# A two-layer attention kernel: v made with seven block products instead of eight

## The chip, the cores and the metric

The kernel runs on one core of a Trainium2 chip. The metric is the device time of one execution in microseconds, the median of three runs.

## The reference

x has the shape (16, 256, 32, 32) in float32: 16 images, C = 256 channels, N = 32 x 32 = 1024 positions. Two layers follow each other, and each adds to x what an attention over the positions makes of the normalised x:

```
x = x + attention(groupnorm(x), Wq, bq, Wk, bk, Wv, bv, rel_h, rel_w)

q, k, v = W @ xf + b                      # xf: (256, 1024); 4 heads of d = 64
sim  = einsum('bhdi,bhdj->bhij', q, k)
qpos = einsum('hdi,bhdj->bhij', rel_h + rel_w, q)
out  = einsum('bhdn,bhmn->bhdm', v, softmax(sim + qpos))
```

The normalisation takes 16 groups along the last axis, over channels and width. Everything is computed in float32.

## The kernel before, in words

A *unit* is one image in one layer; there are 32, in an order that interleaves the two layers. A unit has two pairs of heads (`pr`), and a pair has two halves of 512 queries, so a unit has four *blocks*, called b = 0 to 3 here. `block(n)` (L803) issues the instructions of one block on all engines, in an order written out by hand; each engine runs its own instructions in that order. Blocks with even b also make the projections that come next: b = 0 makes q, k and the second half of v for the unit's own second pair of heads (`w` is the same unit), b = 2 makes q, k and the first half of v for the next unit. A block does this:

- Eight groups of *scores* j = 0 to 7 (`scores`, L549): a tile of 128 keys by 2 heads by 512 queries, four matmuls of 64 rows by 64 columns that use the four quarters of TensorE together. Ahead of each, VectorE writes the *seed* (`seed`, L513), the positional term, into the two PSUM banks that the scores add to. Behind it, ScalarE takes the exponential out of the banks into p (`scores`, L560 and L562).
- The product of p with v (`attend`, L602) in two stretches, one from the lower and one from the upper rows. Its groups j = 0 to 3 read `vts[u, 0]`, j = 4 to 7 read `vts[u, 1]`. `take_out` (L663) copies the result out of PSUM.
- The sums of p over the keys: VectorE adds p tiles into `first` and `acc` (`add_up`, L567, L582), and DMAs that accumulate, issued on GpSimd's queue, add and fold those (`add_first` L619, `fold` L624, `fold_again` L643, `fold_stack` L648, first<-p L578).
- `finish` (L720, L727) normalises an older pair's output and adds it to x.

The PSUM has eight banks, used as four pairs "a" to "d"; `ring` names them `ta, tb, tx, tz` in each block. In an even block `tz` holds q and k, `tx` holds v until it is copied, and the seeds go round over the pairs.

q and k are made together with seven block products instead of eight (`first_product` L360, `two_products` L409) after Winograd's form of Strassen's scheme: the weights' sums are built once (`forms`), the sums of the normalised input x_n once a unit (`input_sums`, L344 to L351). v is made in the plain way: `values` (L445), 64 products of 64 rows by 256 columns a unit, in two stretches of each even block; ScalarE copies them out (L470). A second stretch waits for the end of the first one on TensorE itself (`stretches`). `norms` issues ScalarE's share of the next units' normalisation after tables (`APPLY`, `SQUARES`, `SUMS`), in pieces between the exponentials.

## Time and profile before

| What | Value |
|---|---|
| Median of 3 runs | 2478.74 us (2478.73 to 2479.44) |
| The profiled execution | 2479.26 us, span 2477.5 us |
| TensorE busy | 2467.9 us (100%) |
| VectorE busy | 2350.6 us (95%) |
| ScalarE busy | 2076.5 us (84%) |
| GpSimd busy | 795.7 us (32%) |
| Granted TensorE clock | 0.999 |

A busy time counts the stretches in which at least one instruction of the engine ran; matmuls are pipelined, so the distance from one group's start to the next one's says more than the length of a record. A float32 matmul leaves two records. Weight loads (PEld) run beside matmuls. A record's start on VectorE can lie up to 0.1 us ahead of the end of the one before it. In a row of a timeline stand the start, the length, the engine, the line, the operation, what it writes and reads, and how many instructions were merged; in brackets the idle time ahead of it and what ended it.

### The profile page before, as it was taken

The numbers are of one execution on the slowest core, as the hardware profiler recorded it, in microseconds if no ns is written. First come the engines' busy times: TensorE is split into PE (matmuls) and PEld (weight loads), VectorE is DVE, ScalarE is ACT, GpSimd is POOL, SyncE is SP. The second block draws the span as 40 slices with busy tenths as digits, with TensorE's granted clock in tenths as the row PEclk, the third lists the DMA queues.
The fourth block names the chain that finished last, engine by engine and source line by source line (L and its number), as shares of the span: only waits on it lengthen the run. The fifth ranks groups of instructions, "written<-read, shape, count | busy, mean of one in ns | idle before, by whom it ended". The sixth has DMA issues, their size and how long they took to land.

```text
span 2477.5 us, 86516 instructions
## 1 busy us (share of the span) xinstructions
PE 2467.9 (100%) x37030; PEld 1825.8 (74%) x37030; DVE 2350.6 (95%) x2815; ACT 2076.5 (84%) x4341; POOL 795.7 (32%) x942
## 2 busy tenths in 40 slices
PE   9999999999999999999999999999999999999998
PEld 5777777777777777777777777777777777777785
DVE  8899999999999999999999999999999999999998
ACT  8888888898888888888888889888888888888764
POOL 0233333333333333333333333333333333333231
PEclk9999999999999999999999999999999999999999
DMA  3655655657557566565575665665656656556564
GB/s 95 115 104 98 129 96 114 119 118 144 112 115 144 105 116 118 108 137 112 113 133 108 125 119 99 130 134 109 129 118 135 116 93 131 112 96 121 106 129 116
DMA packets 138551, 289.25 MB, mean 117 GB/s; under 512 B 55848, under 2 KB 57384, under 8 KB 138160
## 3 DMA queue, kind: packets, MB, share of 16 engines
q0 software_dynamic: 72288, 197.74, 47.3%
q1 hardware_dynamic: 65584, 85.38, 11.6%
q8 instruction: 293, 4.80, 0.8%
q14 instruction: 98, 0.80, 0.1%
q10 hardware_dynamic: 288, 0.52, 0.1%
HBM read 51.78 MB, written 17.30 MB: 28 GB/s over the span
## 4 chain that ended last, share of the span: by engine, by line
PE 98%; DVE 1%; ACT 1%; DMA 0%; issue 0%; SPq 0%; PEldq 0%; ACTq 0%
PE banks L549 36%; PE banks L602 35%; PE banks L409 13%; PE banks L445 9%; PE banks L486 2%; PE banks L360 2%; PE banks L317 0%; PE banks L240 0%; DVE banks L513 0%; DMA x<-in_x_dram 0%; ACT p L562 0%; PE banks L675 0%; ACT xn L296 0%; ACT junk L221 0%; DVE r L1121 0%
## 5 line engine op out<-in xcount | busy, mean ns | idle before, releaser
L513 DVE TENSOR_TENSOR banks<-abt 128x1024 f32<-128x1024 f32 x1207 | 1241.2, 1061 | 93.3 <-ACT p L562 49.2
L562 ACT ACTIVATE p<-banks,shift 128x1024 f32<-128x1024 f32 x898 | 981.4, 1116 | 202.5 <-PE banks L549 104.6
L549 PE MATMUL banks<-q,k 64*64 64x512 f32 x8192 | 1068.9, 590 | 0.5 <-DVE banks L513 0.4
L602 PE MATMUL banks<-p,v 64*64 64x256 f32 x16384 | 951.6, 376 | 0.0
L602 PEld LDWEIGHTS banks<-p,v 64*64 64x64 f32 x16384 | 838.5, 133 | 120.4 <-issue 39.1
L549 PEld LDWEIGHTS banks<-q,k 64*64 64x64 f32 x8192 | 466.2, 133 | 281.8 <-issue 153.7
L582 DVE TENSOR_TENSOR acc<-acc,p 128x1024 f32<-128x1024 f32 x381 | 465.2, 1221 | 4.3
L648 POOL DMA_DIRECT2D stack<-stack x310 | 308.2, 994 | 316.8 <-DMA stack<-stack 148.7
L409 PE MATMUL banks<-t,form 64*64 64x512 f32 x1984 | 399.7, 589 | 0.0
L643 POOL DMA_DIRECT2D stack<-acc x248 | 241.6, 1186 | 471.2 <-DMA stack<-acc 458.0
L445 PE MATMUL banks<-Wv,xn 64*64 64x256 f32 x3968 | 293.5, 378 | 0.0
L409 PE MATMUL banks<-xn,form 64*64 64x512 f32 x992 | 258.8, 589 | 0.0
L445 PEld LDWEIGHTS banks<-Wv,xn 64*64 64x64 f32 x3968 | 228.9, 133 | 40.2 <-PEq L199 16.8
L619 POOL DMA_DIRECT2D acc<-first x126 | 115.1, 914 | 423.1 <-DVE acc L582 224.3
L296 ACT ACTIVATE xn<-x,nshift,rstd 128x128 f32<-128x128 f32 x496 | 209.3, 500 | 30.1 <-DVE nshift L289 30.1
L221 ACT ACTIVATE junk<-x,neg 128x128 f32<-128x128 f32 x501 | 199.7, 407 | 0.0
L560 ACT ACTIVATE p<-banks,shift 128x512 f32<-128x512 f32 x252 | 159.8, 685 | 35.3 <-PE banks L549 32.3
L409 PEld LDWEIGHTS banks<-t,form 64*64 64x64 f32 x1984 | 137.8, 133 | 67.8 <-issue 41.8
L624 POOL DMA_DIRECT2D acc<-acc x124 | 103.3, 833 | 254.5 <-DMA acc<-first 251.4
L578 POOL DMA_DIRECT2D first<-p x127 | 114.1, 899 | 179.2 <-ACT abt L499 66.8
L567 DVE TENSOR_TENSOR acc<-p,p 128x1024 f32<-128x1024 f32 x128 | 156.2, 1220 | 0.4 <-DMA acc<-first 0.4
L567 DVE TENSOR_TENSOR first<-p,p 128x1024 f32<-128x1024 f32 x127 | 154.7, 1218 | 0.0
(120 smaller groups left out, 1776.6 us busy)
## 6 DMA issues: line engine op xcount, KB each, us to landing
first<-p POOLq DMA_DIRECT2D x127, 512.0 KB, 6.8
acc<-first POOLq DMA_DIRECT2D x126, 512.0 KB, 5.5
rden<-rd SPq DMA_DIRECT2D x126, 256.0 KB, 6.7
acc<-acc POOLq DMA_DIRECT2D x124, 256.0 KB, 5.9
stack<-acc SPq DMA_DIRECT2D x248, 64.0 KB, 2.9
stack<-acc POOLq DMA_DIRECT2D x248, 64.0 KB, 3.4
out_dram<-x SPq DMA_DIRECT2D x31, 512.0 KB, 2.9
x<-in_x_dram SPq DMA_DIRECT2D x30, 512.0 KB, 9.5
```

Of the source, the lines that this page charges most:

```text
L221: nc.scalar.activation(junk, grouped(xt[units[u][0]], g), func, accum_out=into[:, g : g + 1], **bias)
L296: nc.scalar.activation(grouped(xns[u], g), grouped(xt[units[u][0]], g), AF.Identity, bias=shift[:, g : g + 1], scale=rstd[:, g : g + 1],)
L409: yield nc.tensor.matmul(ps[c, a, :], f[rs, left[a], c0 : c0 + D], right[a][rs, :], start=(t == 0 and step == 1 and a == 1), stop=(t == 1) ...
L445: yield nc.tensor.matmul(pv[c, a, i, :], xns[u][rs, cc, j0 : j0 + D], W.wv[l][rs, cc, :], start=(t == 0 and cc == 0 and i == 0), stop=(t = ...
L513: nc.vector.tensor_tensor(ps[:, h].rearrange("p h (w y) -> p h w y", y=H), ab[:, h, :H].unsqueeze(2).to_broadcast(shape), ab[:, h, H + hal ...
L549: nc.tensor.matmul(ps[c, h, :], a[hs, j0 : j0 + D], b[hs, columns], start=bool(tag) and i == 0, stop=i == len(terms) - 1, skip_group_check ...
L562: nc.scalar.activation(p, ps, AF.Exp, bias=W.shift)
L567: nc.vector.tensor_tensor(t, probs[blk, a], probs[blk, b], ALU.add)
L582: nc.vector.tensor_tensor(accs[blk], accs[blk], probs[blk, j], ALU.add)
L602: yield nc.tensor.matmul(po[c, a, :QUART], vts[u, j // 4][rs, j % 4, c0 : c0 + D], p[rs, h, a * QUART : (a + 1) * QUART], start=(fresh and ...
L643: nc.gpsimd.dma_start(at, acc[R:D, h, :], accum_op=ALU.add)
L648: nc.gpsimd.dma_start(stack[:rows_], stack[rows_ : 2 * rows_], accum_op=ALU.add)
```

## The change

v, too, is made with seven products of blocks of 128 rows. The sums of the weights stand in `vform`, built once a layer by `value_forms`; the sums of the input are those that q and k have already. The products are made in pairs, `value_pair`, and the first one, `odd_products`, together with q's and k's first product. A matmul of v now has 128 columns instead of 256, and there are 112 a unit instead of 64. b = 2 makes the first product and a pair (48 matmuls), b = 0 two pairs (64).

The results need five additions a unit. Two, which read PSUM, are VectorE's: into c22 in b = 0 and into c11 in b = 2. Three are GpSimd's `tensor_tensor`, SBUF only, all in b = 0: into c22, into c12 and into u2; for the last one ScalarE copies a bank into a part of x_n that is no longer read. c12 is read by the product with p of the same block, groups j = 4 to 7; c22 and u2 belong to the second pair of heads and are read two blocks later.

The order in `block` changes around these. The second pair's stretches stand between scores 3, 4 and 5. `tx` holds v longer, so seeds 3 to 6 take turns in `ta` and `tb`, seed 7 goes to `tx`, and p's product with v to `ta`. The exponential of scores 4 is one instruction instead of two halves. The first sum of p (`add_up(blk, 1)`) comes behind v's addition and seed 4. The first sum of the input in b = 2 goes to the head of the block, and the tables `APPLY` and `SQUARES` move pieces of normalisation to later places. The spread reciprocals have one buffer instead of two, to make room.

The core of the diff:

```diff
-            first = None if plain else first_product(w, pr, qk)
-            v, v_out = values(w, 1 - b // 2, psum2(tx, f"pv_{w}_{b}"), first)
+            pv = psum2(tx, f"pv_{w}_{b}")
+            if plain:
+                v, v_out = values(w, 1, pv)
+            elif b == 0:
+                new_values(w, 1)
+                v = value_pair(w, 1, pv, first_product(w, pr, qk))
+            else:
+                v = odd_products(w, pr, qk, pv)
...
-            add_up(blk, 1)
             v(1)
+            if b == 2:
+                new_values(w, 0)
+                nc.scalar.copy(value_block(w, 0, 0), bank_of(pv, 0))
+                after_first(w, pr, qk)
+            elif plain:
+                v_out()
+            else:
+                c22, u2 = value_block(w, 1, 1), value_block(w, 0, 1)
+                nc.scalar.copy(c22, bank_of(pv, 0))
...
-            v_out()
+            seed(blk, 4, tb)
+            if b == 0 and not plain:
+                nc.vector.tensor_tensor(c22, c22, bank_of(pv, 1), ALU.add)
+                nc.gpsimd.tensor_tensor(c22, c22, u2, ALU.add)
+            add_up(blk, 1)
             if n > 0:
                 scores(blk, 3)
-            seed(blk, 4, tb)
...
+                v = value_pair(w, 2 - b, pv)
+            if b == 0:
+                products(0)
+            if not plain:
+                v(0)
+            seed(blk, 5, ta, halves=True)
+            scores(blk, 4)
+            if not plain:
+                v(1)
+            if b == 2:
+                c11 = value_block(w, 0, 0)
+                nc.vector.tensor_tensor(c11, c11, bank_of(pv, 1), ALU.add)
+                nc.scalar.copy(value_block(w, 0, 1), bank_of(pv, 0))
+                products(0)
+            elif not plain:
+                c12 = value_block(w, 1, 0)
+                part = bank_of(xns[w][:, :, :HALF], 0)
+                nc.scalar.copy(c12, bank_of(pv, 0))
+                nc.gpsimd.tensor_tensor(c12, c12, u2, ALU.add)
+                nc.scalar.copy(part, bank_of(pv, 1))
+                nc.gpsimd.tensor_tensor(u2, u2, part, ALU.add)
             norms(u, b, 1)
-            seed(blk, 5, tx, halves=True)
-            scores(blk, 4, halves=True)
-            seed(blk, 6, ta)
+            scores(blk, 5)
+            seed(blk, 6, tb)
+            products(1)
             if folded:
                 stack_up(previous)
-            scores(blk, 5)
-            products(1)
-            po = psum2(tx, f"po_{n}")
+            po = psum2(ta, f"po_{n}")
             zeroed(po)
-            seed(blk, 7, tb, halves=True)
+            seed(blk, 7, tx, halves=True)
...
-    APPLY = {0: (3, 7, 7, 7, 7, 7), 1: (7, 7, 7, 11, G, G)}
+    APPLY = {0: (3, 3, 3, 7, 7, 7), 1: (7, 7, 7, 11, G, G)}
```

Three places show the new order. TensorE at the head of a block b = 0 before, from the first product (L360) on; `Wv` rows are v, `q,k` rows are scores 2, 3 and then 4 and 5, `form` rows are q and k:

```order
L360 MATMUL banks<-xn_16334,form_76 64x512 x2
L445 MATMUL banks<-Wv_78,xn_16334 64x256 x12
L360 MATMUL banks<-xn_16334,form_76 64x512 x2
L445 MATMUL banks<-Wv_78,xn_16334 64x256 x4
L549 MATMUL banks<-q_0_16928,k_0_16929 64x512 x4
L445 MATMUL banks<-Wv_78,xn_16334 64x256 x16
L549 MATMUL banks<-q_0_16928,k_0_16929 64x512 x4
L409 MATMUL banks<-t_16851,form_76 64x512 x2
L409 MATMUL banks<-xn_16334,form_76 64x512 x2
L549 MATMUL banks<-q_0_16928,k_0_16929 64x512 x8
```

The same place in the changed kernel, where `vform` rows are v:

```order
L377 MATMUL banks<-xn_15228,form_76 64x512 x2
L457 MATMUL banks<-vform_78,t_15772 64x128 x12
L377 MATMUL banks<-xn_15228,form_76 64x512 x2
L457 MATMUL banks<-vform_78,t_15772 64x128 x4
L631 MATMUL banks<-q_0_15833,k_0_15834 64x512 x4
L457 MATMUL banks<-vform_78,t_15772 64x128 x16
L631 MATMUL banks<-q_0_15833,k_0_15834 64x512 x4
L426 MATMUL banks<-t_15772,form_76 64x512 x2
L426 MATMUL banks<-xn_15228,form_76 64x512 x2
L457 MATMUL banks<-vform_78,xn_15228 64x128 x2
L457 MATMUL banks<-vform_78,t_15772 64x128 x2
```

Ahead of scores 2 and 3 stand the same numbers of v's matmuls with half the columns; the other pair now follows ahead of scores 4 and 5, which used to come together.

VectorE at that place before, from the last addition of the older block on; `abt` rows are seeds 3, 4, 5 (halves), 6, 7 (halves):

```order
L582 TENSOR_TENSOR acc_1_1_9703<-acc_1_1_9703,p_1_1_7_9667 128x1024
L513 TENSOR_TENSOR banks<-abt_0_9701 128x1024
L567 TENSOR_TENSOR first_0_0_9858<-p_0_0_0_9747,p_0_0_1_9823 128x1024
L513 TENSOR_TENSOR banks<-abt_0_9701 128x1024
L513 TENSOR_TENSOR banks<-abt_0_9701 128x512 x2
L513 TENSOR_TENSOR banks<-abt_0_9701 128x1024
L513 TENSOR_TENSOR banks<-abt_0_9701 128x512 x2
L720 TENSOR_TENSOR od_1_8654<-od_1_8654,rden_1_9650 128x1024
```

And in the changed kernel:

```order
L664 TENSOR_TENSOR acc_1_1_10207<-acc_1_1_10207,p_1_1_7_10171 128x1024
L595 TENSOR_TENSOR banks<-abt_0_10205 128x1024 x2
L962 TENSOR_TENSOR v_1_10322<-v_1_10322,banks 128x4x128
L649 TENSOR_TENSOR first_0_0_10387<-p_0_0_0_10251,p_0_0_1_10327 128x1024
L595 TENSOR_TENSOR banks<-abt_0_10205 128x512 x2
L595 TENSOR_TENSOR banks<-abt_0_10205 128x1024
L595 TENSOR_TENSOR banks<-abt_0_10205 128x512 x2
L807 TENSOR_TENSOR od_1_9105<-od_1_9105,rden_1_10154 128x1024
```

Seed 3 keeps its place; seed 4 moves ahead of the first sum, and v's addition (L962) stands between them.

GpSimd's queue in a block b = 0 before, from `add_first` (L619) to `fold_again` (L643):

```order
L619 DMA acc_1_1_11577<-first_1_1_11534 128x1024
L648 DMA stack_0_11168<-stack_0_11168 8x512
L578 DMA first_0_0_11732<-p_0_0_2_11730 128x1024
L624 DMA acc_1_1_11577<-acc_1_1_11577 64x1024
L648 DMA stack_0_11168<-stack_0_11168 4x512
L643 DMA stack_1_11627<-acc_1_0_11414 32x512 x2
L643 DMA stack_1_11627<-acc_1_1_11577 32x512 x2
```

And in the changed kernel:

```order
L701 DMA acc_1_1_11197<-first_1_1_11154 128x1024
L730 DMA stack_0_10772<-stack_0_10772 8x512
L706 DMA acc_1_1_11197<-acc_1_1_11197 64x1024
L730 DMA stack_0_10772<-stack_0_10772 4x512
L725 DMA stack_1_11246<-acc_1_0_11034 32x512 x2
L963 TENSOR_TENSOR v_1_11311<-v_1_11311,v_0_10860 128x4x128
L660 DMA first_0_0_11376<-p_0_0_2_11345 128x1024
L994 TENSOR_TENSOR v_1_11311<-v_1_11311,v_0_10860 128x4x128
L996 TENSOR_TENSOR v_0_10860<-v_0_10860,xn_10278 128x4x128
L725 DMA stack_1_11246<-acc_1_1_11197 32x512 x2
```

The three additions (into c22, c12 and u2) stand behind the folds of the older block, and the first sum's DMA has moved from ahead of the fold to between the additions.

More of the change, by code (lines that the diff above doesn't have):

```diff
@@ L435, in k_half, with value_part, odd_products, products @@
         )
+    def value_part(u, ps, rs, a, form, right, i, start=False, stop=False):
+        for x, c in enumerate(QUARTERS):
+            p0 = i * P + x * D
+            yield nc.tensor.matmul(
+                ps[c, a, i * P : (i + 1) * P], right[rs, p0 : p0 + D],
+                W.vform[units[u][1]][rs, form, :],
+                start=start and i == 0, stop=stop, skip_group_check=True,
+            )
+    def odd_products(u, pr, qk, pv):
+        f = W.form[units[u][1]]
+        def products(t):
+            mine, other = ((LO, HI), (HI, LO))[t]
+            for i in range(NT // 2):
+                yield from value_part(u, pv, mine, 0, A11, xb(u, 0, 0), i, t == 0, t == 1)
+                if i == 0:
+                    for h, c in enumerate(QUARTERS):
+                        c0 = pr * P + h * D
+                        yield nc.tensor.matmul(
+                            qk[c, 0, :], f[other, A11, c0 : c0 + D], xb(u, 0, 0)[other, :],
+                            start=t == 0, stop=t == 1, skip_group_check=True,
+                        )
+        return stretches(products)
+    def value_pair(u, step, pv, first=None):
+        left, right = (
+            ((S2, A12), (ts[u][:, T2], xb(u, 1, 0))),
+            ((S1, S3), (ts[u][:, T1], ts[u][:, T3])),
+            ((S4, NA22), (xb(u, 1, 1), ts[u][:, T4])),
+        )[step]
+        fresh = (1, 0, 2)[step]
+        def products(t):
+            rounds = [
+                [
+                    value_part(
+                        u, pv, rs, a, left[a], right[a], i, t == 0 and a >= fresh, t == 1
+                    )
+                    for rs, a in BANKS[t]
+                ]
+                for i in range(NT // 2)
+            ]
+            if t == 0 and first is not None:
+                yield from woven(rounds, first)
+            else:
+                for r in rounds:
+                    for p in r:
+                        yield from p
+        return stretches(products)
+    def value_block(u, nh, ch):
+        return vts[u, nh][:, :, ch * P : (ch + 1) * P]
+    def bank_of(ps, a):
+        return ps[:, a, :].rearrange("p (b c) -> p b c", c=P)
+    def new_values(u, g):
+        vts[u, g] = vpool.tile([P, NT // 2, C], F32, tag="v", name=f"v_{u}_{g}")
     def values(u, g, pv, first=None):
@@ L820, in block @@
         ta, tb, tx, tz = ring
+        if even and b == 2:
+            input_sums(w, 0)
         if previous and even:
```

65 lines of the change are left out of this document (44 added, 21 removed).

## The prediction

> **What bounds the kernel now.** I read the page first, then busy time by windows, then the timelines of TensorE (PE), VectorE (DVE), ScalarE (ACT) and GpSimd (POOL) over one steady unit. Busy times, then shares of the chain that ended last:
>
> ```profile
> PE 2467.9 (100%) x37030; PEld 1825.8 (74%) x37030; DVE 2350.6 (95%) x2815; ACT 2076.5 (84%) x4341; POOL 795.7 (32%) x942
> PE 98%; DVE 1%; ACT 1%; DMA 0%; issue 0%; SPq 0%; PEldq 0%; ACTq 0%
> ```
>
> TensorE is the path, and VectorE is right behind it. In a steady window (columns: length, then busy us of PE, PEld, DVE, ACT, POOL):
>
> ```profile
> 1100.00:1400.00 300.00, 300.00 (x4532) 223.28 (x4528) 287.05 (x338) 257.30 (x547) 101.18 (x119) 1.00 0.61 117
> ```
>
> DVE is idle 12.95 us in 300, and the granted clock is 1.00. Now TensorE at the start of a block b=0 (first L360 at 1022.09), then of the b=2 block after it (1060.23); L549 are scores, L445 v, L602 the product with p:
>
> ```profile
> 1021.23 1.07 PE L549 MATMUL banks<-q,k 64*64 64x512 f32 x8
> 1022.09 0.63 PE L360 MATMUL banks<-xn,form 64*64 64x512 f32 x2
> ...
> 1024.67 1.13 PE L549 MATMUL banks<-q,k 64*64 64x512 f32 x8
> 1025.53 2.00 PE L445 MATMUL banks<-Wv,xn 64*64 64x256 f32 x32
> 1027.26 1.13 PE L549 MATMUL banks<-q,k 64*64 64x512 f32 x8
> ...
> 1028.97 1.99 PE L549 MATMUL banks<-q,k 64*64 64x512 f32 x16
> ...
> 1033.27 1.07 PE L602 MATMUL banks<-p,v 64*64 64x256 f32 x14
> ```
>
> ```profile
> 1060.23 0.63 PE L360 MATMUL banks<-xn,form 64*64 64x512 f32 x2
> ...
> 1062.81 1.13 PE L549 MATMUL banks<-q,k 64*64 64x512 f32 x8
> ...
> 1065.40 1.13 PE L549 MATMUL banks<-q,k 64*64 64x512 f32 x8
> ...
> 1071.40 1.46 PE L602 MATMUL banks<-p,v 64*64 64x256 f32 x21
> ```
>
> From start to start, a group of scores takes 0.86 (1024.67 to 1025.53), 32 v records take 1.73 (to 1027.26), and the woven stretch with the first product takes 2.58 (1022.09 to 1024.67). Two blocks are 38.14, so a unit is 76.28, and of that DVE idles 3.3 (76.28 x 12.95/300).
>
> **The change, term by term.** *TensorE.* v has 112 products of 128 columns in a unit for 64 of 256: 7/8 of the columns. In b=0 it stays at two pairs, in two places instead of one; in b=2 it falls by a quarter of the former v, one slot of 0.86. Do 128-column products run at the column rate? The nearest row is shorter still:
>
> ```profile
> 1012.55 0.93 PE banks L486 x61
> ```
>
> A stretch of 64 records of 64 columns takes 0.93, 14.5 ns each; 32 of 128 columns need 0.86, 27 ns each, so issue doesn't limit them. Removed: 0.86 a unit, in 31 units 26.7 us, if nothing else gets late.
>
> *The VectorE total.* Rows by form:
>
> ```profile
> L513 DVE TENSOR_TENSOR banks<-abt 128x1024 f32<-128x1024 f32 x829 | 1002.5, 1227 | 91.9 <-ACT p L562 49.2 <-ACT od L663 41.0 <-ACT abt L499 1.0
> L513 DVE TENSOR_TENSOR banks<-abt 128x512 f32<-128x512 f32 x378 | 246.1, 697 | 1.4 <-ACT v L470 0.9 <-ACT p L560 0.5
> L433 DVE SCALAR_TENSOR_TENSOR k<-banks,bk,k 128x512 f32<-128x512 f32 x124 | 87.2, 703 | 0.0
> L470 ACT COPY v<-banks 128x512 f32<-128x512 f32 x128 | 68.8, 590 | 37.0 <-PE banks L445 37.0
> L562 ACT ACTIVATE p<-banks,shift 128x1024 f32<-128x1024 f32 x898 | 981.4, 1116 | 202.5 <-PE banks L549 104.6 <-DVE rstd L276 83.4 <-PE banks L602 3.3
> ```
>
> The two additions read PSUM and SBUF as L433 does: 2 x 0.70 = 1.4. Of 3.3 idle 1.9 is left, less the 0.86 that the unit would shrink by: 1.0. In total VectorE still fits; what decides is where its work is due.
>
> *Seeds, b=0.* Every group of scores needs a seed that VectorE wrote into its banks. VectorE there:
>
> ```profile
> 1024.85 1.23 DVE L513 TENSOR_TENSOR banks<-abt 128x1024 f32<-128x1024 f32 x1
> 1025.99 1.22 DVE L567 TENSOR_TENSOR first<-p,p 128x1024 f32<-128x1024 f32 x1
> 1027.12 2.43 DVE L513 TENSOR_TENSOR banks<-abt 128x1024 f32<-128x1024 f32 x3
> 1029.70 2.47 DVE L513 TENSOR_TENSOR banks<-abt 128x1024 f32<-128x1024 f32 x3
> 1032.08 1.22 DVE L720 TENSOR_TENSOR od<-od,rden 128x1024 f32<-128x1024 f32 x1
> ```
>
> Seed 3 ends at 1024.85 + 1.23 = 1026.08, and nothing ahead of it on VectorE changes. Scores 3 were due at 1027.26. Both v stretches ahead of them now lose 0.86, so they are due at 1025.53. With about 0.1 for the handover they start at 1026.2: 0.7 late. The products of the second pair now lie behind them, so scores 4 start three slots later, at 1028.8. The second pair of v also keeps the third pair of banks until it is copied, so seeds 3 to 6 alternate over two pairs, and seed 6 must wait for the exponential of scores 4. That wait shows in ACT's idle time:
>
> ```profile
> 1022.36 1.12 ACT L562 ACTIVATE p<-banks,shift 128x1024 f32<-128x1024 f32 x1 [0.27 <-PE banks L549]
> ...
> 1025.87 1.12 ACT L562 ACTIVATE p<-banks,shift 128x1024 f32<-128x1024 f32 x1 [0.25 <-PE banks L549]
> ```
>
> The exponential starts 1.13 to 1.20 after its scores (1021.23, 1024.67). VectorE meanwhile: seed 4 to 1027.4, v's addition (0.7), the first sum (1.22) and seed 5 to 1030.3, with the overlaps of 0.1 between records; scores 5 are due at 1030.5, so those just fit, and VectorE then idles 0.8. On the path instead: scores 4 at 1028.8, exponential 1029.97 to 1031.09, seed 6 to 1032.35. Scores 6, four slots of 0.86 behind scores 4, are due at 1032.2 and start at 1032.45. Seed 7 in halves (0.70 each, overlapping by 0.1) ends at 1033.55; scores 7 were due at 1033.3 and start at 1033.65. The product with p starts at 1034.5 instead of 1033.27: **+1.2 us** (bounds 0.7, the first wait alone, and 1.6, if v's addition, which now waits for a copy on ScalarE with the first sum and seed 5 queued behind it, also makes scores 5 late).
>
> *Seeds, b=2.* VectorE there:
>
> ```profile
> 1062.01 1.22 DVE L513 TENSOR_TENSOR banks<-abt 128x1024 f32<-128x1024 f32 x1
> 1063.14 0.68 DVE L349 TENSOR_TENSOR t<-t,xn 128x512 f32<-128x512 f32 x1
> 1063.74 1.22 DVE L567 TENSOR_TENSOR first<-p,p 128x1024 f32<-128x1024 f32 x1
> ...
> 1067.84 2.48 DVE L513 TENSOR_TENSOR banks<-abt 128x1024 f32<-128x1024 f32 x3 [0.20 <-ACT p L562]
> ```
>
> Seed 3 ends at 1063.23. Three slots from 1060.23 put scores 3 at 1062.81 instead of 1065.40; they start at 1063.35, 0.54 late. Seed 4, which moves ahead of the first sum, ends near 1064.97; scores 4 are due at 1065.07. The addition into c11 (0.70) waits for TensorE's second stretch of the pair, with seed 6 queued behind it; it ends at 1067.9 and seed 6 at 1069.05, with scores 6 due at 1069.37. Nine slots from 1063.35 end at 1071.1; with 0.1 at scores 7 the product with p starts at 1071.2 instead of 1071.40: **-0.2 us** of the 0.86 (bounds -0.5 and +0.1).
>
> *What costs nothing.* ScalarE has one more copy (0.59) a unit and two exponentials whole instead of in halves; by the windows' row it idles 42.70 in 300, 10.9 a unit, which covers it. The normalisations that leave the start of b=0 and b=2 only make room ahead of the exponentials; if they landed in front of one instead, each would cost what it delays. The sum of inputs that moves ahead of an addition on VectorE in b=2 leaves seed 3 where it is. The forms of v are some ten small instructions, once: 1 us. Reciprocals' spread with one buffer on SP's queue waits for a multiplication one block earlier, so nothing queues behind it. The sum's DMA on GpSimd, now issued some 5 us later, is next needed a block later.
>
> *GpSimd's additions.* No row shows one. The bounds are 0.69 (VectorE's of that size) and 1.19 (GpSimd's slowest row, below). The one that matters is the addition into c12, which the product with p reads from its fifth group, after 32 records of 256 columns, 1.73 as v's; behind it on TensorE are the next block's first scores. GpSimd's queue at b=0, and the page's row of its fold:
>
> ```profile
> 1031.49 0.82 POOL L624 DMA_DIRECT2D acc<-acc  x1 [2.84 <-DMA acc<-first]
> 1032.02 1.13 POOL L648 DMA_DIRECT2D stack<-stack  x1
> 1032.56 2.34 POOL L643 DMA_DIRECT2D stack<-acc  x2
> ```
>
> ```profile
> L643 POOL DMA_DIRECT2D stack<-acc x248 | 241.6, 1186 | 471.2 <-DMA stack<-acc 458.0 <-issue 13.2
> ```
>
> Both additions of b=0 and the first-sum DMA are now queued behind these. From between 1033.75 (one row's mean behind the start) and 1034.90, with additions of 0.69 to 1.19 and a DMA issue of 0.54 (the pace of these rows) to 0.82, c12 is ready between 1035.7 and 1038.1; it is needed at 1034.5 + 1.73 = 1036.2. I take nothing for it, nearer to the early end: the 2.84 of waiting at L624 is for a transfer that ran beside the first sum's, and that one now goes out behind it. 1.5 stays for the range.
>
> **Sum.** 31 x (1.2 - 0.2) + 1 = +32 on the profiled execution's 2479.26 (span 2477.5 and 1.76 around it; 0.5 above the median 2478.74). On the median: **2510 us**. This case's own range: 31 x 0.2 to 31 x 1.7, 2486 to 2532.
>
> **Rivals.** *VectorE is held while GpSimd adds.* The three additions fall where VectorE runs seed 7, the normalisation and the next seeds, all with two inputs from SBUF. If such instructions can't run beside an addition of GpSimd, VectorE loses 3 x (0.69 to 1.19) = 2.1 to 3.6 a unit, at a place where it is already late; the cushion behind it is its wait for the copy of the output:
>
> ```profile
> DVE banks L513 <- ACT od L663: 41.0, 60, 1.1
> ```
>
> That is 41.0/60 = 0.7 a time, so 1.4 to 2.9 stay on top of the forecast: 2510 + 43 to 2510 + 90, 2553 to 2600, middle 2576. For it: VectorE's rows stand end to end there. Against it: VectorE's sums keep their length beside GpSimd's DMA work, though that isn't an addition (min, median, max ns):
>
> ```profile
> L582 DVE TENSOR_TENSOR acc<-acc,p x381: 1212/1220/1227, 48.9 to 2449.9; 128x1024 f32<-128x1024 f32 x191
> ```
>
> Chance 0.28. The Trainium skill states such a rule (SBUF — State Buffer, § Who interferes with whom): a VectorE instruction with two SBUF inputs and a GpSimd instruction that reads SBUF exclude each other for a whole instruction. By that rule the time is about 2576; the trace of before has no addition on GpSimd and can't show it. The same skill (GPSIMD Engine Reference, § Performance versus the Vector engine) gives 4497 ns for 2048 elements, by which I estimate 1.1 us for 512.
>
> *c12 comes late.* No holding, but the queue above keeps the product with p waiting 0.5 to 1.5 in each b=0: 2525 to 2556. Chance 0.12.
>
> *Faster.* If seed 3 were ready at 1025.5 and 1062.8, TensorE would keep its order without waits and the whole 0.86 stays: 2478.7 - 26.7 + 1 = 2453. This decides from seeds 0.7 and 0.54 earlier than the trace has them; VectorE's 3.3 idle speaks for it, the unchanged order ahead of seed 3 against it. Partial gains reach 2473. Chance 0.19. *A draw:* the waits come to 0.86, half of the 1.2 + 0.66 that I count, and the time to 2474 to 2484; chance 0.10. That the change doesn't do what it says is out: its matmuls are there in the built order.
>
> **Chances and range.** Forecast 0.31, held VectorE 0.28, late c12 0.12, faster 0.19, draw 0.10. A measurement here can tell about 0.2%, 5 us, from no change. Faster 0.19, same 0.10, slower 0.71. The range from 2460 to 2590 leaves out half of the faster case (0.1) and the upper quarter of the held one (0.07).
>
> **What would show it.** Right: TensorE's wait for L595's seeds at scores 3 of both even blocks, 0.7 and 0.5; an idle VectorE of some 0.8 before seed 6 of b=0; a unit of 77.3. Held VectorE: records of seeds or sums of over 1.5 us beside GpSimd's TENSOR_TENSOR. Late c12: TensorE or its weight loads waiting for v's L994. Wrong: a unit of 75.4 and no wait for seeds.

## The result and the profile after

| | Before | After |
|---|---|---|
| Median | 2479.05 us | 2686.39 us |
| Ratio, with its 95% interval | | 1.083 (1.082 to 1.085) |
| TensorE busy | 2467.9 us (100%) | 2573.9 us (96%) |
| VectorE busy | 2350.6 us (95%) | 2534.0 us (94%) |
| GpSimd busy | 795.7 us (32%) | 946.5 us (35%) |

One of the four executions of the changed kernel took 2926.2 us at a granted clock of 0.873 and is left out of the ratio, though not of the median; the other three took 2685.3 to 2687.5.

The kernel became 207 us slower, where 32 were forecast. First the page's busy times and the chain that ended last, by engine:

```profile
PE 2573.9 (96%) x40006; PEld 1690.9 (63%) x40006; DVE 2534.0 (94%) x2885; ACT 2073.2 (77%) x4313; POOL 946.5 (35%) x1035
PE 76%; DVE 17%; ACT 4%; issue 2%; DMA 1%; POOL 1%; SPq 0%; DVEq 0%; PEldq 0%; POOLq 0%; ACTq 0%
```

VectorE had 1% of the chain and has 17%. It has 70 instructions more than before, the 62 additions of 0.68 us being worth 42 us, but it is busy 183 us longer. The waits say where TensorE meets it, at the seeds ahead of the scores (us in total, times, longest):

```profile
PEld banks L631 <- DVE banks L595: 275.0, 435, 4.3
PE banks L631 <- DVE banks L595: 77.7, 50, 3.5
```

Before, the weight loads waited 80.9 us for seeds, at most 1.1 at a time:

```profile
PEld banks L549 <- DVE banks L513: 80.9, 263, 1.1
```

The groups by form show that not every VectorE instruction got longer:

```profile
L595 DVE TENSOR_TENSOR banks<-abt 128x512 f32<-128x512 f32 x378 | 341.4, 950 | 0.1
L807 DVE TENSOR_TENSOR od<-od,rden 128x1024 f32<-128x1024 f32 x62 | 103.6, 1672 | 0.0
L962 DVE TENSOR_TENSOR v<-v,banks 128x512 f32<-128x512 f32 x31 | 21.1, 681 | 0.0
L987 DVE TENSOR_TENSOR v<-v,banks 128x512 f32<-128x512 f32 x31 | 21.2, 685 | 0.1
```

The seed in halves has a mean of 950 ns (697 before), the normalisation 1672 (1219, below). Both read two inputs from SBUF. The two new additions, which read one input from PSUM, take 681 and 685, as forecast (0.70); none of them runs beside an addition on GpSimd.

```profile
L720 DVE TENSOR_TENSOR od<-od,rden 128x1024 f32<-128x1024 f32 x63 | 76.8, 1219 | 0.0
```

GpSimd's three additions are new; their rows give the shortest, the median and the longest:

```profile
L963 POOL TENSOR_TENSOR v<-v,v x31: 1607/2517/2997, 118.9 to 2605.3; 128x512 f32<-128x512 f32 x31
L994 POOL TENSOR_TENSOR v<-v,v x31: 1660/2907/4062, 120.7 to 2607.2; 128x512 f32<-128x512 f32 x31
L996 POOL TENSOR_TENSOR v<-v,xn x31: 1602/1604/2153, 124.3 to 2610.1; 128x512 f32<-128x512 f32 x31
```

An addition that runs by itself takes 1.60 us; my bounds had been 0.69 and 1.19. Most take longer than that, and so do VectorE's records beside them. One block b = 0, whose first product starts at 1025.98, shows the two side by side. VectorE (seeds 6 and 7, the normalisation):

```profile
1035.38 6.39 DVE L595 TENSOR_TENSOR banks<-abt 128x1024 f32<-128x1024 f32 x3 [0.87 <-ACT p L644]
1041.68 2.28 DVE L807 TENSOR_TENSOR od<-od,rden 128x1024 f32<-128x1024 f32 x1
```

GpSimd in the same stretch:

```profile
1036.36 2.36 POOL L963 TENSOR_TENSOR v<-v,v 128x512 f32<-128x512 f32 x1
...
1038.29 2.91 POOL L994 TENSOR_TENSOR v<-v,v 128x512 f32<-128x512 f32 x1
1041.27 1.60 POOL L996 TENSOR_TENSOR v<-v,xn 128x512 f32<-128x512 f32 x1
```

And TensorE, from scores 6 on (L631 are scores, L684 the product with p):

```profile
1036.66 1.09 PE L631 MATMUL banks<-q,k 64*64 64x512 f32 x8
1040.15 1.07 PE L631 MATMUL banks<-q,k 64*64 64x512 f32 x2 [2.40 <-DVE banks L595]
1041.82 0.65 PE L631 MATMUL banks<-q,k 64*64 64x512 f32 x3 [0.59 <-DVE banks L595]
1041.84 0.64 PE L684 MATMUL banks<-p,v 64*64 64x256 f32 x2
...
1042.32 5.08 PE L684 MATMUL banks<-p,v 64*64 64x256 f32 x53
```

Three seed records (one whole, two halves) that take 2.44 us elsewhere take 6.39 here, while two additions run. The first half of seed 7 comes at 1040.1 and the second at 1041.8, and scores 7, due at 1037.5, wait for both. Then the first stretch of the product with p, whose 64 records take 3.6 to 3.8 us in other blocks, takes over 5 for 53 of them. The windows of 2 us say why (the value behind the five engines is the granted clock):

```profile
1038.00:1040.00 2.00, 0.00 (x0) 0.00 (x0) 2.00 (x1) 0.99 (x1) 2.00 (x3) 1.00 0.26 34
1040.00:1042.00 2.00, 1.25 (x6) 0.37 (x10) 2.00 (x3) 0.00 (x0) 1.92 (x2) 1.00 1.05 197
1042.00:1044.00 2.00, 2.00 (x22) 1.02 (x22) 1.97 (x2) 0.73 (x1) 0.88 (x1) 0.61 0.50 77
1044.00:1046.00 2.00, 2.00 (x28) 1.38 (x24) 2.00 (x2) 2.00 (x8) 0.64 (x2) 0.54 0.24 66
1046.00:1048.00 2.00, 2.00 (x42) 1.63 (x38) 2.00 (x3) 2.00 (x12) 1.06 (x2) 1.00 0.41 48
```

After the idle stretch the clock falls to 0.61 and 0.54 and is back at 1.00 from 1046. Over the whole execution the mean clock is 0.979 where it was 0.999:

```profile
core 0: 2683.4 us, clock 0.979
```

Where the time goes can be read from distances on TensorE. From the start of a b = 2 block to the next b = 0 (the pair of blocks from b = 2) it is now 37.65 us (38.14 before): 0.49 is won. From the start of b = 0 to the next b = 2 (the pair from b = 0) it is 44.9 in the middle (43.3 to 47.7; 38.14 before): 6.7 is lost. So all of the loss lies in b = 0 and the block behind it. This table holds, for b = 0, the start of each group of scores and of the product with p, in us behind the first product (medians over the units, from the records of each trace; the forecast's are worked out from the times in the prediction):

| | scores 3 | 4 | 5 | 6 | 7 | product with p | next b = 2 |
|---|---|---|---|---|---|---|---|
| before | 5.17 | 6.89 | 7.75 | 9.46 | 10.32 | 11.18 | 38.14 |
| forecast | 4.1 | 6.7 | 8.4 | 10.4 | 11.6 | 12.4 | 39.3 |
| after | 3.92 | 6.95 | 8.69 | 10.68 | 14.17 | 15.86 | 44.9 |

Up to scores 6 the forecast holds within 0.3 us. It breaks at scores 7, whose seed stands beside GpSimd's additions.

### The profile page after: what moved, and what is told of

The parts are those of the page before. It is cut to its first block, busy times and chain, and to the rows that moved or that the text cites. A ratio compares the mean times of both kernels' runs of the same rounds, so it can differ in the third digit from the quotient of the medians.

```text
span 2683.4 us, 92697 instructions
## 1 busy us (share of the span) xinstructions
PE 2573.9 (96%) x40006; PEld 1690.9 (63%) x40006; DVE 2534.0 (94%) x2885; ACT 2073.2 (77%) x4313; POOL 946.5 (35%) x1035
## 4 chain that ended last, share of the span: by engine, by line
PE 76%; DVE 17%; ACT 4%; issue 2%; DMA 1%; POOL 1%; SPq 0%; DVEq 0%; PEldq 0%; POOLq 0%; ACTq 0%
PE banks L631 29%; PE banks L684 29%; DVE banks L595 10%; PE banks L426 10%; PE banks L457 4%; ACT p L644 4%; DVE acc L664 3%; PE banks L568 2%; DVE t L361 1%; PE banks L377 1%; DVE v L962 1%; DVE od L807 1%; DMA acc<-first 0%; PE banks L334 0%; PE banks L257 0%
## 5 line engine op out<-in xcount | busy, mean ns | idle before, releaser
L595 DVE TENSOR_TENSOR banks<-abt 128x1024 f32<-128x1024 f32 x1207 | 1353.8, 1154 | 114.1 <-ACT p L644 82.6
L644 ACT ACTIVATE p<-banks,shift 128x1024 f32<-128x1024 f32 x961 | 1054.2, 1115 | 450.8 <-PE banks L631 351.6
L631 PE MATMUL banks<-q,k 64*64 64x512 f32 x8192 | 1196.9, 603 | 80.2 <-DVE banks L595 77.7
L684 PE MATMUL banks<-p,v 64*64 64x256 f32 x16384 | 1028.0, 384 | 12.0 <-POOL v L994 12.0
L684 PEld LDWEIGHTS banks<-p,v 64*64 64x64 f32 x16384 | 810.5, 136 | 209.2 <-issue 80.2
L631 PEld LDWEIGHTS banks<-q,k 64*64 64x64 f32 x8192 | 388.7, 133 | 451.9 <-DVE banks L595 275.0
L457 PE MATMUL banks<-vform,t 64*64 64x128 f32 x3968 | 235.2, 272 | 7.1 <-DVE v L962 5.9
L457 PEld LDWEIGHTS banks<-vform,t 64*64 64x64 f32 x3968 | 198.3, 132 | 55.6 <-ACT v L946 18.1
L457 PEld LDWEIGHTS banks<-vform,xn 64*64 64x64 f32 x2976 | 171.1, 133 | 75.2 <-issue 33.8
L660 POOL DMA_DIRECT2D first<-p x127 | 177.3, 1396 | 105.6 <-ACT abt L581 63.4
L457 PE MATMUL banks<-vform,xn 64*64 64x128 f32 x2976 | 203.0, 271 | 0.7 <-ACT od L745 0.5
```

What stands on the lines that cost most here:

```text
L457: yield nc.tensor.matmul(ps[c, a, i * P : (i + 1) * P], right[rs, p0 : p0 + D], W.vform[units[u][1]][rs, form, :], start=start and i == 0, ...
L595: nc.vector.tensor_tensor(ps[:, h].rearrange("p h (w y) -> p h w y", y=H), ab[:, h, :H].unsqueeze(2).to_broadcast(shape), ab[:, h, H + hal ...
L631: nc.tensor.matmul(ps[c, h, :], a[hs, j0 : j0 + D], b[hs, columns], start=bool(tag) and i == 0, stop=i == len(terms) - 1, skip_group_check ...
L644: nc.scalar.activation(p, ps, AF.Exp, bias=W.shift)
L660: nc.gpsimd.dma_start(firsts[blk], probs[blk, 2], accum_op=ALU.add)
L684: yield nc.tensor.matmul(po[c, a, :QUART], vts[u, j // 4][rs, j % 4, c0 : c0 + D], p[rs, h, a * QUART : (a + 1) * QUART], start=(fresh and ...
```

## The experiments

The theory after this: *VectorE held*. An addition on GpSimd and a VectorE instruction with two inputs from SBUF exclude each other, seed 7 comes late, and TensorE's idle time then costs a stretch at half clock. The rivals: the new turns of the seeds are the whole loss, whoever adds (*seeds alone*); the product with p waits for c12 (*late c12*); VectorE simply has too much to do (*too little time*). The runs of each comparison had the kernel before beside them, at 2479.2 to 2479.9 us.

**Without the three additions.**

```diff
-                nc.gpsimd.tensor_tensor(c22, c22, u2, ALU.add)
...
-                nc.gpsimd.tensor_tensor(c12, c12, u2, ALU.add)
...
-                nc.gpsimd.tensor_tensor(u2, u2, part, ALU.add)
```

> The changed kernel with GpSimd's three additions left out (c22, c12 and u2 lack their last term); all else stays. Theory, VectorE held: GpSimd's additions hold VectorE's two-input instructions, and the late seed 7 leaves TensorE idle until its clock is halved; without them only the late seeds of b = 0 stay: 2495 to 2515 us, no seed record over 1.3 us, granted clock 0.999, the block pair from b = 0 near 39.3 us instead of 44.75. Rival, seeds alone: the turns of the seeds over two pairs of banks are the whole loss, whoever adds: 2650 or more. Rival, late c12: only the four waits for c12 go, 12 us in all: about 2674.

Measured: 2523.4 us, ratio 1.017 (1.016 to 1.019). The mean clock, the seeds in halves, and the normalisation:

```profile
core 0: 2523.7 us, clock 0.999
L595 DVE TENSOR_TENSOR banks<-abt 128x512 f32<-128x512 f32 x378 | 244.6, 693 | 0.0
L807 DVE TENSOR_TENSOR od<-od,rden 128x1024 f32<-128x1024 f32 x62 | 75.5, 1218 | 0.0
```

The additions cost 163 us of the 207; the seeds and the clock are as before without them. Seeds alone (2650 or more) and late c12 (2674) fall. What stays, 44 us, is more than I expected, and the time lies 8 us above the range: the pair from b = 0 takes 39.78 instead of 39.3. The starts in the table's order are 3.91, 6.95, 8.69, 10.68, 11.59 and 12.45 for the product with p. So 1.27 of the loss lies ahead of that product, where 1.2 was forecast, and 0.37 behind it. One wait in it was not in my list: v's second pair must wait until VectorE's addition into c22 has read the bank that it writes.

```profile
PEld banks L457 <- DVE v L962: 13.4, 31, 0.7
PE banks L457 <- DVE v L962: 5.9, 31, 0.4
```

**The additions on VectorE**, at the same places.

```diff
-                nc.gpsimd.tensor_tensor(c22, c22, u2, ALU.add)
+                nc.vector.tensor_tensor(c22, c22, u2, ALU.add)
```

(and so for the other two)

> The changed kernel with the three additions on VectorE instead of GpSimd, at the same places. Theory, VectorE held: an addition costs VectorE its own 0.6 to 0.7 us there instead of the 1.6 us for which GpSimd's holds it; 1.9 us a unit more than without the additions, of which up to 1.0 is covered: 2525 to 2570 us, clock 0.99 or more. Rival, VectorE has too little time: whatever is added at this place makes seed 7 late in the same way; 2 us more on VectorE instead of none bring 2686 or more.

Measured: 2580.6 us, ratio 1.041 (1.039 to 1.042), clock 0.999. Two of the additions, as groups:

```profile
L994 DVE TENSOR_TENSOR v<-v,v 128x512 f32<-128x512 f32 x31 | 21.5, 692 | 19.1 <-ACT v L993 19.1
L996 DVE TENSOR_TENSOR v<-v,xn 128x512 f32<-128x512 f32 x31 | 21.5, 692 | 3.6 <-DVE v L994 0.5
```

The same additions cost 57 us on VectorE and 163 on GpSimd. VectorE has 2.1 us a unit more to do there than with nothing (3 x 0.69), and the pair from b = 0 is 1.96 longer (41.74 against 39.78): almost nothing of it is covered, and the time lies 11 us above the theory's range. So VectorE is full at this place, as the rival says, but 2 us more of work on it do not bring the 2686 that the rival needs.

**The additions in the kernel before.** Three additions per b = 0 into a part of x_n that is not read any more, behind the second pair of q and k.

```diff
             products(1)
+            if b == 0 and not plain:
+                for _ in range(3):
+                    nc.gpsimd.tensor_tensor(xb(w, 0, 0), ts[w][:, T1], ts[w][:, T3], ALU.add)
             po = psum2(tx, f"po_{n}")
```

> The kernel before with three additions of 128x512 on GpSimd in each block b = 0, from two sums of inputs into a part of x_n that nobody reads any more; nothing waits for them, and the result is the same. Theory, VectorE held: three additions of 1.6 us hold VectorE for up to 4.8 us a unit, of which its idle time of 3.3 a unit covers a part: between 1 and 5 us a unit, 2510 to 2630 us, and seed records of 1.5 us and more beside the additions. Rival, no holding: nothing waits for GpSimd, so 2479 to 2484 us and all seeds at 1.22 and 0.70.

Measured: 2563.7 us, ratio 1.034 (1.032 to 1.036). Nothing in the program waits for these additions, and the rest is the kernel before, with the same order:

```profile
L513 DVE TENSOR_TENSOR banks<-abt 128x1024 f32<-128x1024 f32 x829 | 1068.8, 1310 | 59.4 <-ACT p L562 44.7 <-ACT od L663 13.0 <-ACT abt L499 1.0
L882 POOL TENSOR_TENSOR xn<-t 128x512 f32<-128x512 f32 x93 | 209.8, 2256 | 4.9
```

The additions' mean is 2.26 us and the whole seeds got 66 us longer (1068.8 against 1002.5). The price of three additions that nobody needs is 84 us here, 2.7 a unit, with VectorE idle 3.3 a unit and the clock at 0.998. TensorE waits for seeds there (52.3 us on the matmuls, 0.4 before) and for no DMA of GpSimd's queue. This shows the hold by itself, with no waits of the change around it.

**TensorE kept busy.** 16 matmuls with zero weights, added to banks of the same unit's q and k, between scores 6 and 7 of b = 0.

```diff
             scores(blk, 6)
+            if b == 0 and not plain:
+                for rs, a in [x for _ in range(4) for x in BANKS[1]]:
+                    for c in QUARTERS:
+                        nc.tensor.matmul(
+                            qk[c, a, :], zero[rs, :], xb(w, 1, 0)[rs, :],
+                            start=False, stop=True, skip_group_check=True,
+                        )
             if before:
```

The first kernel made for this had the zeros but, by a slip, not the matmuls:

> The changed kernel with 16 more matmuls (weights zero, added to banks of the same product of q and k) between scores 6 and 7 of b = 0, some 3.4 us of TensorE work, where it idles for seed 7. The result is the same. Theory, halved clock: the idle time of 3.5 to 4 us is followed by 3.4 us at half clock, about 2 us a unit lost; with TensorE kept busy the clock stays near 1.00 and the time falls to 2610 to 2650 us although there is more work. Rival, the clock is without weight: the idle time only takes up the work, 2680 to 2695. Rival, the work does not fit the idle time: up to 3.4 us a unit on top, up to 2790 us.

It is therefore a second run of the changed kernel: 2686.0 us, ratio 1.084, clock 0.980. With the matmuls in it:

> The changed kernel with 16 matmuls of zero weights (3.4 us of TensorE work at full clock, added to banks of the same unit's q and k; the result is the same) between scores 6 and 7 of each b = 0, where TensorE idles for seed 7. The run before it lacked these matmuls and was a second run of the changed kernel. Theory, halved clock: the idle time there is followed by 3.4 or 6.8 us at half clock, 1.7 to 2 us a unit; with TensorE busy instead the clock stays near 1.00 and the time falls to 2615 to 2645 us although there is more work. Rival, the clock is without weight: the idle time only takes up the work, 2680 to 2695. Rival, the work doesn't fit the idle time: up to 3.4 us a unit on top, up to 2790.

Measured: 2664.5 us, ratio 1.074 (1.073 to 1.076). The mean clock, and TensorE at one such place:

```profile
core 0: 2661.9 us, clock 0.998
1024.82 1.09 PE L635 MATMUL banks<-q,k 64*64 64x512 f32 x8
1025.72 3.61 PE L1014 MATMUL banks<-xn,zero 64*64 64x512 f32 x32
1029.16 1.04 PE L635 MATMUL banks<-q,k 64*64 64x512 f32 x8
1030.02 3.63 PE L688 MATMUL banks<-p,v 64*64 64x256 f32 x64
```

With 3.4 us more of work in every b = 0 the kernel is 22 us faster, so the clock has weight, and the product with p takes 3.6 again. The fall is smaller than I expected: the range ended at 2645.

How much of the 163 us is the clock? In 31 units the clock record of the changed kernel's trace has 24 stretches at half clock, each of 3.41 or 6.83 us. Half of their length, 53 us, is what TensorE missed; the mean clock gives the same, (0.999 - 0.979) x 2683 = 54. Not all of that made the kernel longer. Of 30 pairs from b = 0, 7 have no such stretch; they take 43.8 us on average (43.3 to 44.4), and all 30 take 45.07. That makes at most 1.25 x 31 = 39 us for the clock, at most because the pairs with a stretch at half clock have mostly the later seed 7 too. The reason shows in TensorE's waits: in each of the 7 it waits 1.0 to 1.4 us for a seed in the block behind, since VectorE is late there anyhow, and in none of the other 23.

In the run with the matmuls the pair takes 44.40 on average, 0.6 more than the 7 pairs at full clock: the matmuls don't fit everywhere, since scores 7 come at another time in each unit. That is 18 us, so that the 22 us gained are what the clock gave back less what the matmuls cost; the clock's share is therefore at least 22. So of the 163 us of the additions I estimate 22 to 39 as halved clock. The other 124 to 141, 4.0 to 4.5 a unit, are the hold; 12 us of waits for c12 are in them.

**Does a GpSimd instruction hold VectorE by writing, or by reading?** Three memsets, then three copies, in place of the three additions; all three stand where the last addition stood, and the other two lines go.

```diff
-                nc.gpsimd.tensor_tensor(u2, u2, part, ALU.add)
+                for _ in range(3):
+                    nc.gpsimd.memset(part, 0.0)
```

> The changed kernel with three memsets of 128x512 on GpSimd in each b = 0 in place of its three additions (c22, c12 and u2 lack their last term): GpSimd writes, but reads nothing. Theory, held by reads: only an instruction of GpSimd that reads SBUF holds VectorE's two-input instructions, so 2518 to 2530 us as without additions (2523), all seeds at 1.22 and 0.70. Rival, held by any work of GpSimd: each memset of some 0.5 us or more holds VectorE as the additions do, 2560 or more, with seeds over 1.5 us.

Measured: 2520.5 us, ratio 1.016 (1.015 to 1.018); the run without additions had 1.017. Seeds in halves and the memsets (shortest, median, longest):

```profile
L595 DVE TENSOR_TENSOR banks<-abt 128x512 f32<-128x512 f32 x378 | 244.3, 691 | 0.0
L995 POOL MEMSET xn<- x93: 525/526/2164, 119.6 to 2455.0; 128x512 f32 x93
```

Writing costs VectorE nothing: 31 whole seeds ran beside a memset in this trace, and none took over 1.24. Some memsets themselves took up to 2.2 us. Then the copies:

```diff
-                nc.gpsimd.tensor_tensor(u2, u2, part, ALU.add)
+                for _ in range(3):
+                    nc.gpsimd.tensor_copy(part, u2)
```

> The changed kernel with three copies of 128x512 on GpSimd, SBUF to SBUF, in each b = 0 in place of its three additions (c22, c12 and u2 lack their last term): one input is read instead of two. Theory, held by reads: a GpSimd instruction that reads SBUF, even with one input, holds VectorE's instructions with two inputs from SBUF; seeds or normalisations of over 1.5 us beside the copies, and for copies of some 0.8 to 1.6 us each 2540 to 2660 us. Rival, held by two-input instructions alone: as with the memsets, 2518 to 2530 us, seeds at 1.22 and 0.70.

Measured: 2544.4 us, ratio 1.026 (1.025 to 1.028).

```profile
L595 DVE TENSOR_TENSOR banks<-abt x1207: 684/1225/1635, 20.2 to 2515.2; 128x1024 f32<-128x1024 f32 x119, 128x512 f32<-128x512 f32 x54
L995 POOL COPY xn<-v x93: 613/1502/3268, 119.2 to 2469.5; 128x512 f32<-128x512 f32 x93
```

The longest seed is 1635 ns, 0.41 over its 1225, and the normalisation takes up to 2009, 0.79 over its 1216. A copy alone takes 0.61 us and a memset 0.53, so the length is not what tells them apart: the instruction that reads holds VectorE, the one that only writes does not. An addition alone takes 1.60, and three of them cost 163 us (124 or more without the clock) where three copies cost 21. The Trainium skill has this rule (SBUF — State Buffer, § Who interferes with whom): a VectorE instruction with two SBUF inputs contends with a GpSimd instruction that reads SBUF, and not with one that only writes it. The runs agree with it: no hold with memsets, a short one with copies, a long one with additions. Whether a VectorE instruction with one input from SBUF is spared isn't shown, since none ran beside an addition in the steady units.

**The additions as accumulating DMAs** on GpSimd's queue, as the sums of p are made.

```diff
-                nc.gpsimd.tensor_tensor(c12, c12, u2, ALU.add)
+                nc.gpsimd.dma_start(c12, u2, accum_op=ALU.add)
```

(and so for the other two)

> The changed kernel with the three additions as accumulating DMAs on GpSimd's queue, as the sums of p have them; the result is the same. Theory, held by additions: no engine's instruction adds, so 2518 to 2535 us as without the additions, seeds at 1.22 and 0.70, clock 0.999. Rival, late c12: the DMA into c12 stands behind others in the queue and lands some 3 to 5 us after its issue, when the product with p is already at its fifth group: 1 to 3 us a unit more, 2555 to 2615, with TensorE waiting for a DMA into v at the product with p.

Measured: 2844.6 us, ratio 1.148 (1.146 to 1.150), the worst of all. The waits of the product with p, and the clock:

```profile
PEld banks L684 <- DMA v<-v: 255.9, 31, 9.5
PE banks L684 <- DMA v<-v: 241.8, 31, 9.1
core 0: 2839.6 us, clock 0.950
```

The rival is right and its price was too low: TensorE waits for c12 in every one of 31 units, 241.8 / 31 = 7.8 us on the matmuls, and the clock falls to half behind it (0.50 from 1010 to 1018 us in one unit, 0.950 in the mean). The start of scores 7 (11.59) is that of the run without additions, so there is no hold; the transfer is late instead. A next kernel moved two steps on VectorE as well:

> As the run with the additions as accumulating DMAs, with two steps moved on VectorE in b = 0: seed 3 ahead of the older block's last sum, and the addition out of PSUM into c22 ahead of seed 4. The result is the same. Theory: without the additions the loss in b = 0 is scores 3 waiting 0.47 us for seed 3 and the second pair of v waiting 0.45 us for c22's addition to leave its bank; with both gone a unit is 0.9 us shorter, 2490 to 2505 us. Rival, the seeds from 4 on bound it: seed 4 now ends 0.6 later and scores 4 and 6 follow it, so that nothing is won: 2518 or more.

Measured: 2842.1 us, ratio 1.148 (1.143 to 1.153). It put seed 3 into banks that scores 1 still needed, so that its scores 1 and 3 were computed from other seeds, and the wait for c12 covers whatever else it did. Nothing about seeds follows from it.

**Seed 3 early, without additions.** In the right place, behind scores 1 in the program:

```diff
-        if previous and even:
-            add_up(previous, 7)
...
                 seed(blk, 3, ta)
+            if previous:
+                add_up(previous, 7)
...
```

> The changed kernel with the three additions left out (c22, c12 and u2 lack their last term) and seed 3 ahead of the older block's last sum on VectorE in b = 0 and b = 2, in the place of the run whose early seed 3 went into banks that scores 1 still read (so that its scores 1 and 3 were others). Theory, late seed 3: scores 3 wait 0.47 us in b = 0 and 0.54 us in b = 2 for it; with both gone a unit is up to 1.0 us shorter than without the additions alone (2523): 2490 to 2508 us. Rival, seed 4 bounds b = 0: it waits for the exponential of scores 2 and holds scores 4 whenever seed 3 comes, so only b = 2 gains: 2505 to 2515. Rival, nothing gained: 2520 to 2526.

Measured: 2547.6 us, ratio 1.028 (1.026 to 1.030): slower than with the late seed 3, which no theory expected. In b = 0 scores 3 come at 3.48 instead of 3.91, and scores 4 at 6.95 as ever; the pair stays 39.79. So seed 3 is not what bounds b = 0, and the rival is right that seed 4 does, by one step more than it says: c22's addition stands behind seed 4 on VectorE and ends 6.18 behind the first product in this run as in the one without additions, and v's second pair, ahead of scores 4, waits for it 13.2 us in all where it waited 5.9. In b = 2 scores 3 come at 2.63 instead of 2.87, but scores 4 at 5.51 instead of 4.65, and the pair takes 38.55 instead of 37.65. VectorE around the start of such a block, at 1011.06, shows the reason (the seeds here are 3 and 4):

```profile
1010.38 1.22 DVE L361 TENSOR_TENSOR t<-xn 128x1024 f32<-128x1024 f32 x1
1012.41 1.23 DVE L595 TENSOR_TENSOR banks<-abt 128x1024 f32<-128x1024 f32 x1 [0.81 <-ACT p L644]
1013.55 1.22 DVE L664 TENSOR_TENSOR acc<-acc,p 128x1024 f32<-128x1024 f32 x1
1014.69 0.68 DVE L366 TENSOR_TENSOR t<-t,xn 128x512 f32<-128x512 f32 x1
1015.29 1.23 DVE L595 TENSOR_TENSOR banks<-abt 128x1024 f32<-128x1024 f32 x1
```

Seed 3 waits 0.81 for the exponential that frees its banks. The sum used to fill that time; now it comes behind, and seed 4 ends 5.45 behind the block's start instead of 4.55. 0.9 x 31 = 28 us, of which 24 were measured.

**All sums, without an addition on GpSimd.** c22 and c12 are added by VectorE straight out of PSUM, u2 by a DMA a block later; seed 3 as in the last run, the first sum behind seed 5.

```diff
-                nc.scalar.copy(c12, bank_of(pv, 0))
-                nc.gpsimd.tensor_tensor(c12, c12, u2, ALU.add)
+                nc.vector.tensor_tensor(c12, bank_of(pv, 0), u2, ALU.add)
...
+                nc.vector.tensor_tensor(c22, bank_of(pv, 0), u2, ALU.add)
                 nc.vector.tensor_tensor(c22, c22, bank_of(pv, 1), ALU.add)
...
+                nc.gpsimd.dma_start(u2, part, accum_op=ALU.add)
```

> The whole computation, without an addition on GpSimd: c22 and c12 are made by VectorE straight from PSUM (each bank plus u2, in place of a copy on ScalarE and a GpSimd addition), u2's by an accumulating DMA one block later, where nothing waits for it; seed 3 goes ahead of the older block's last sum and the first sum behind seed 5. Theory, held VectorE: with no hold and no late DMA only the two more VectorE instructions of 0.68 us stay, 1.4 us a unit at most on top of the run with seed 3 early and no additions, less what fits into VectorE's waits: 2480 to 2530 us, all seeds at 1.22 and 0.70, clock 0.999. Rival, the accumulating DMA alone: any more DMA on GpSimd's queue delays the sums and folds there, so that the time stays over 2600, with VectorE or TensorE waiting for DMAs into acc or v.

Measured: 2550.2 us, ratio 1.029 (1.027 to 1.030), which is 20 us over the expected range. The pairs are 39.86 and 38.55: the first is 0.07 above, the second the same as in the run before this one, which left the additions out. So the whole set of sums, with the new order of b = 0, costs 0.07 us a unit in this form. Of the 71 us above the kernel before, 44 are there without any addition on GpSimd, 24 come with the early seed 3, and 3 with the sums. The two additions out of PSUM, which replace copies on ScalarE:

```profile
L962 DVE TENSOR_TENSOR v<-banks,v 128x512 f32<-128x512 f32 x31 | 21.4, 692 | 11.6 <-PE banks L457 11.6
L997 DVE TENSOR_TENSOR v<-banks,v 128x512 f32<-128x512 f32 x31 | 21.2, 683 | 0.0
```

**Another order in b = 0.** As the last one, with b = 2 as in the changed kernel.

```diff
                 products(0)
+            if b == 0 and not plain:
+                products(1)
+                scores(blk, 4)
+                v(0)
+                v(1)
+                seed(blk, 5, ta, halves=True)
+                seed(blk, 6, tb)
...
```

> The whole computation, as in the run with VectorE's additions straight from PSUM and one DMA, but b = 2 as in the changed kernel, and b = 0 in another order: both stretches of the second q and k pair ahead of scores 4, then both stretches of v's second pair, seeds 5 and 6 ahead of c12's addition, the first sum behind seed 7. Theory, late seeds: without holds the rest of the loss in b = 0 (39.79 against 38.14 us) is scores 4, which stand behind v's second pair and that behind seed 4 and c22's addition; with TensorE given the q and k stretch in that time the product with p starts 11.5 to 11.8 us behind the first product (12.45 without the additions, 11.18 before), a unit takes 76.2 to 76.7, and the time is 2478 to 2500 us. Rival, VectorE is out of time: what TensorE no longer waits for there it waits for at seeds 5 to 7, since VectorE has the same work; 2515 to 2530. Well below 2478 is what neither expects.

Measured: 2545.3 us, ratio 1.026 (1.025 to 1.028). The pair from b = 2 is back at 37.64. That from b = 0 takes 40.53, and scores 4 to 7 come at 6.80, 9.82, 10.68 and 11.67, the product with p at 12.73. Both theories miss: the time lies 15 us over the rival's range too. Seed 4 ended 5.6 behind the first product and did not hold scores 4. TensorE did: a second stretch waits for the end of the first on TensorE itself, and now the two stretches of both pairs stand back to back, so that scores 4 come 0.7 later than the work ahead of them would let them. The weight loads of q's and k's second pair waited 54.5 us for TensorE's own queue (14.7 in the run without additions), up to 1.1 a time:

```profile
PEld banks L426 <- PEq L216: 54.5, 119, 1.1
```

The pair is 0.67 longer than in the run before: 0.2 of that lies ahead of the product with p, 0.47 behind it. Where the 0.47 come from is not shown.

No version tried beats the kernel before. The one that I would expect to be the best with v's seven products, the last but one with b = 2 as in the changed kernel, was not run; if its pairs were 39.86 and 37.65, they would make 77.5 against 76.28.

## Why the prediction was wrong

**What bounds the kernel: right.** TensorE was the path with VectorE right behind it, and the loss went through seeds.

**The gain on TensorE and the seeds' waits: right in kind, a quarter too small.** 0.86 a unit left b = 2, and the pair there became 0.49 shorter; forecast was 0.2, with bounds of -0.1 to 0.5. In b = 0 the product with p comes 1.27 later without the additions; forecast was 1.2. The single steps are in the table above: scores 3 come at 3.9 (4.1 forecast), scores 6 at 10.68 (10.4). Left out were the wait of v's second pair for c22's bank and 0.37 a unit in the block behind. By the run without additions this part is +44 us where +32 was taken; the middle units make 36 of it, and single units, up to 2.4 us longer, the rest.

**The failed step: "GpSimd's additions".** It bounded one addition by 0.69 and 1.19 us and took nothing for all three but a possible late c12. Measured is 1.60 us for one alone, which lies outside the bounds: the rows that I took were a VectorE addition and a DMA issue, and neither is an addition on GpSimd. And the effect was in the other place. c12 made TensorE wait in 4 of 31 units, 12.0 us in all on the matmuls:

```profile
PE banks L684 <- POOL v L994: 12.0, 4, 3.5
```

The hold, which I had as a rival with a chance of 0.28, was the main thing: at least 124 of the 207 us. My reason against it, sums of VectorE that keep their length beside GpSimd's DMA work, was true and said nothing about additions: a DMA issue is another kind of instruction. The changed kernel shows the same, its sums at 1.22 where no addition runs. The mechanism was in the list; the rule of the Trainium skill beside it should have outweighed an observation of a different kind of instruction.

**The rival's own price was too low as well.** With 1.60 in place of 0.69 to 1.19 its sum, three additions less 0.7 of cushion, is 4.1 a unit, 127 us, on 2510: 2637. Measured is 4.0 to 4.5 a unit for the hold. What it lacked is the clock, 22 to 39 us, and the 12 us by which the seeds' part was too small. No wait for a seed was over 1.1 us in the trace of before, so no row there showed the price of a longer one. The Trainium skill gives the rule (TensorE: Matmul & The Clock Gate, Part 1): the array falls to half clock after an idle window of about 3.4 us and needs about as long a busy one to come back. The trace agrees in kind: 0.61 and 0.54 in two windows of 2 us after a stretch from 1037.8 to 1041.8 with two matmul records in it, and 1.00 again 4 us later. What such a stretch costs is less than half its length where VectorE is late behind it anyhow, as the pairs without one show.

**The sum as it turned out:** 2479 + 44 (seeds, measured without additions) + 163 (the additions: hold and clock) = 2686. Both terms are measured; the split of the 163, at least 124 for the hold and at most 39 for the clock, is worked out from pairs with and without half clock, and the run with TensorE kept busy sets the clock's lower end, 22.

**What stays open:** what the 0.37 a unit in the block behind b = 0 is made of; how the clock's share divides between 22 and 39 us; why a held seed of 128x1024 has a median of 2.30 us beside the additions put into the kernel before, 1.07 over its 1.23, and not the full 1.60 of an addition more; and what an order with neither the bank's wait nor stretches back to back would give.

## What to carry to other kernels

Before elementwise work is given to an idle GpSimd, look at what VectorE runs at that moment: if it has two inputs in SBUF, GpSimd's reading takes VectorE's time, here more than the same additions on VectorE would have (163 us against 57). An addition that VectorE makes straight out of PSUM in place of ScalarE's copy can cost little (two of them, a DMA and a new order made 0.07 us a unit here). A stall on TensorE of 3 to 4 us is to be priced with the half clock that follows it, as far as nothing else is late in that stretch.

## What the runs showed of the hardware that was not expected

- An addition of 128x512 in float32 took 1.60 us on GpSimd alone, and 0.69 on VectorE with the same operands; a copy 0.61 and a memset 0.53 on GpSimd.
- GpSimd's additions are held as well as VectorE's instructions: two of their medians are 2.5 and 2.9 us where VectorE has seeds and the normalisation, and single ones take up to 4.06.
- Three memsets on GpSimd beside VectorE's seeds cost the kernel nothing (2520.5 us against 2523.4 without), though single ones took up to 2.2 us.
- Of 53 us of full clock that TensorE lost at half clock, at most 39 made the kernel longer, since VectorE was late in those stretches anyhow.
- An accumulating DMA of 128x512 that stood in GpSimd's queue behind others made TensorE wait 7.8 us a unit.
